# R's sums, T2, T3 and the order of the last quads: who computes them and when

## The chip, the cores and the metric

The kernel runs on one core of a Trainium2 chip. Its engines work side by side and follow each other through semaphores: TensorE (PE; its weight loads are listed apart as PEld) multiplies matrices and writes into PSUM, VectorE (DVE), ScalarE (ACT) and GpSimd (POOL) compute element by element, and SyncE (SP) issues most of the transfers between the main memory and SBUF. Each engine takes its instructions strictly in the order in which the program gives them. The metric is the device time of one execution in microseconds, lower being better. For the kernel before it is 489.55 us, the median of three runs (489.38 to 489.99).

## What is computed

128 samples x of 64 channels and 1024 positions each pass through four layers of a modulated convolution, and the input is added again at the end. Cut to its core the reference is

```python
TYPES = ('same', 'upsample', 'same', 'downsample')
BLUR_K = np.array([1., 3., 3., 1.]); BLUR_K /= BLUR_K.sum()

def _layer(x, style, w, b, mw, mb, typ):
    s = style @ mw.T + mb                                # a scale for each sample and input channel
    weight = SCALE * w * s[:, None, :, None]
    demod = lax.rsqrt(jnp.sum(weight * weight, axis=(2, 3)) + EPS)
    weight = weight * demod[:, :, None, None]            # each sample has weights of its own
    if typ == 'same':
        out = jax.vmap(_conv_same)(x, weight) + b[None, :, None]
    elif typ == 'upsample':                              # transposed, stride 2, then a blur
        out = jax.vmap(_conv_up)(x, weight.transpose(0, 2, 1, 3)) + b[None, :, None]
        out = _blur(out, 2.0 * blur_k, (1, 1))
    elif typ == 'downsample':                            # a blur, then stride 2
        out = jax.vmap(_conv_down)(_blur(x, blur_k, (2, 2)), weight) + b[None, :, None]
    return out

out = x
for i, typ in enumerate(TYPES):
    out = _layer(out, style, weights[i], biases[i], mod_w[i], mod_b[i], typ)
return x + out
```

All arithmetic is float32. There is no nonlinearity between the layers.

## The kernel before, in words

**The mathematics.** As the layers are linear, the kernel multiplies them together into one filter of nine taps of 64x64 for each sample, and applies it once. It does so for a *quad* of four samples at a time; 128 samples make 32 quads (NQ). The 128 partitions hold two samples of 64 channels, and two such pairs lie side by side.

**The chain of the weights.** For each quad, TensorE and ScalarE make the filter in three stages. `stage1` (L408; in the loop `stage1_a` and `stage1_b`, L423 and L435) makes S, `stage2` (L522, with `stage2_rest`, L497) makes R, seven blocks of 64 columns, and `stage3` (L628; in the loop `stage3_b` and `stage3_a`, L593 and L615) makes W, the nine taps. After `stage2`, `r_sums` (L587) adds two pairs of R's blocks into slots 7 and 8 of the R tile; the last group of products of `stage3_b` reads these two slots, the other six groups don't. `combine_a` and `combine_b` (L670, L678) form merged taps H from W by five additions with two SBUF inputs (`sum_of`, all with line L663) and the residual's two (L660).

**The convolution.** The input of a quad comes as three planes X (positions by their remainder by three). From X come the differences G (`in_g01`, `in_g2`, L663), from X directly T3 (`in3`, L712), and from G the operands T1 (`in1`, L727), T2 (`in2`, L732) and the pair T0 and T4, called T04 below (`in04`, L741). Five products of 3 groups each (`conv0` to `conv4`, all L754) turn T and W or H into sums in PSUM: conv3 uses T3, conv1 T1, conv2 T2, conv4 and conv0 T04. conv3, conv1 and conv2 of a quad accumulate in one tile psA, and what is between them is read by the others: `copy_m3` (ScalarE, L793) after conv3, `sum1` (VectorE, L663, y) after conv1, `sum2` (VectorE) after conv2. The first step of `sum2` writes into Y, two instructions of L663, on which conv4 accumulates; its second is y (L813). `output` (L831 on ScalarE, L833 on VectorE) scales and adds the bias, `store` (L836) writes out.

**The buffers.** X has two buffers, used by even and odd quads. G has one. T04, T12 (T1 and T2 in one tile) and T3 have two each, R has two.

**The loop.** Four quads go through `early_turn` (q = 0 to 3), then 25 through `turn_of` (q = 4 to 28), then the last three quads are written out by hand. The order is written out for every engine; nothing is scheduled by a planner. In `turn_of(q)` (L1412) three quads are under way: q is finished, n = q + 1 is begun with conv3 and conv1, and for c = q + 2 the filter and the operands are made. A turn's order is: stage2 of c, conv2 of q, R's sums of c, sum2 of q, T3 of n, stage3_b of c, the first merges of n, conv4 of q, stage3_a, the other merges, conv3 of n, T04 of n, G of c, conv0 of q, conv1 of n, sum1 of n, T1 and T2 of c. The first turn of the loop (q = 4, `entry`) differs: there sum2 and conv4 of q stand ahead of R's sums. Small work for later quads is spread over the turns in tables (`EXTRA`, `TABLES`, `SIDE`, L1250 to L1294), tables of scales on GpSimd among it, and a layered computation of the positions near the two ends of each sample, whose last step is `rest3_bias` (L1106).

**Who does what around the change.** R's sums are on VectorE, T1, T2 and T3 in the loop on GpSimd, T04 and G on VectorE. The loads of X for quad c + 1 are issued by SyncE right behind T3 of n, the last reader of that buffer of X. The two that matter most are

```python
1421            conv2(q)
1422            r_sums(c)
1423            sum2(q)
1424            in3(n, eng=nc_g)
...
1473        sum1(n)
1474        in1(c, nc_g)
1475        in2(c, nc_g)
```

Of the kernel before, what the change touches and what calls it, by code (L numbers as in the profile page):

```python
# [50 lines left out]
ALU = mybir.AluOpType  # L51
# [12 lines left out]
def kernel(  # L64
# [9 lines left out]
    nc = tc.nc  # L74
    NP, P, NXC = x.shape
    B = 2 * NP
    NQ = B // 4
    HB = B // 2
    NT = 9
    T, Bo = slice(0, C), slice(C, P)  # L80
    HALF = (T, Bo)

    nc_v, nc_a, nc_g = nc.vector, nc.scalar, nc.gpsimd
# [35 lines left out]
    bb = par_s[:, NM + N1 + NL : PS]  # L119
# [42 lines left out]
    Xe = const.tile([P, B, 8], F32, name="Xe")  # L162
# [423 lines left out]

    def r_sums(q):  # L587
        t = chain[q]
        nc_v.tensor_add(t[:, :, 7:9], t[:, :, 2:6:3], t[:, :, 3:7:3])  # L589

    shared_w = {}

# [69 lines left out]
    def sum_of(out, x, f, y, op=ALU.add):  # L662
        nc_v.scalar_tensor_tensor(out, x, f, y, op0=ALU.mult, op1=op)  # L663
# [22 lines left out]
    NJ = NB + 2  # L686
# [4 lines left out]
    BOTH_PAIRS = slice(0, 2)  # L691
    PAIR = slice(0, 1), slice(1, 2)

    def plane(buf, i, pairs=BOTH_PAIRS):

        at = PL * (2 - i) if i < 3 else PL * 2 + 1
        return buf[:, pairs, at : at + NJ]

    def t_tile(q, tag):
        if (q, tag) not in Ts:  # L700
            Ts[q, tag] = tpool.tile([P, 2, 1 + (tag != "T3"), PL], F32, tag=tag, name=f"{tag}_{q}")
        return Ts[q, tag]

    def g_tile(q):
        if q not in Gs:
            Gs[q] = gpool.tile([P, 2, 3 * PL], F32, tag="G", name=f"G{q}")
        return Xs[q % NX], Gs[q]

    def in3(q, pairs=BOTH_PAIRS, eng=nc_v):
        if q < NQ:  # L710
            X, t = Xs[q % NX], t_tile(q, "T3")
            eng.tensor_sub(t[:, pairs, 0, :NJ], plane(X, 3, pairs), plane(X, 1, pairs))  # L712

    def in_g01(q, pairs=BOTH_PAIRS):
        if q < NQ:
            X, g = g_tile(q)
            sum_of(g[:, pairs, PL:], X[:, pairs, : 2 * PL], 0.5, X[:, pairs, PL:], ALU.subtract)

    def in_g2(q, pairs=BOTH_PAIRS):
        if q < NQ:  # L720
            X, g = g_tile(q)
            sum_of(plane(g, 2, pairs), plane(X, 3, pairs), 0.5, plane(X, 2, pairs), ALU.subtract)

    def in1(q, eng):
        if q < NQ:
            t, g = t_tile(q, "T12"), Gs[q]
            eng.tensor_add(t[:, :, 0, :NJ], plane(g, 2), plane(g, 1))  # L727

    def in2(q, eng):
        if q < NQ:  # L730
            t, g = t_tile(q, "T12"), Gs[q]
            eng.tensor_sub(t[:, :, 1, :NJ], plane(g, 2), plane(g, 1))  # L732

    def in04(q, pairs=BOTH_PAIRS):
        if q < NQ:
            t, g = t_tile(q, "T04"), Gs[q]
            a, b = g[:, pairs, :NJ], g[:, pairs, 2 * PL : 2 * PL + NJ]
            both = lambda v, step: bass.AP(
                v.tensor, v.offset, [*(list(d) for d in v.ap[:-1]), [step, 2], [1, NJ]]
            )  # L740
            nc_v.tensor_sub(t[:, pairs, :, :NJ], both(a, PL), both(b, 1))  # L741

    def product(q, m, ps, groups=range(K)):

        W, H_ = Wq[q]
        tag, i = SLOT[m]
        for g in groups:
            for s, rows in enumerate(HALF):
                for c, cols in enumerate(HALF):
                    if m in (0, 4):  # L750
                        w = W[rows, tap(m // 2, g), c, :]
                    else:
                        w = H_[rows, m - 1, g, c, :]
                    nc.tensor.matmul(  # L754
                        ps[s][cols, :NB],
                        w,
                        Ts[q, tag][rows, c, i, g : g + NB],
                        start=(g == 0 and m == 3),
                        stop=(g == K - 1),
                        skip_group_check=True,  # L760
                    )

    def m_tile(tag, q, bufs=1):
        return mpool.tile([P, 2, NB], F32, tag=tag, name=f"{tag}_{q}", bufs=bufs)
# [3 lines left out]
    def parts(q):  # L768

        if isinstance(A[q], list):  # L770
            return [(slice(s, s + 1), A[q][s][:, None, :NB]) for s in range(2)]
        return [(slice(0, 2), A[q][:, :, :NB])]

    def banks(q):
        return A[q] if isinstance(A[q], list) else [A[q][:, s] for s in range(2)]
# [22 lines left out]
    def sum1(q):  # L798

        y1w[q] = m_tile("y1", q, 2)  # L800
        for s, a in parts(q):
            sum_of(y1w[q][:, s], a, 2.0, m3c[q][:, s])
# [12 lines left out]
    def conv4(q, *groups):  # L815
        product(q, 4, Y_banks, groups or range(K))

    def conv0(q, *groups):
        product(q, 0, banks(q), groups)
# [15 lines left out]
    def store(q, s, planes=slice(0, K), queue=nc.sync):  # L835
        queue.dma_start(  # L836
            out[q, :, s, planes.start * NB : planes.stop * NB],
            os[q][:, s, planes].rearrange("c i j -> c (i j)"),
        )
# [105 lines left out]
    Oe = const.tile([P, B, 3], F32, name="Oe")  # L945
# [17 lines left out]
    def blurred(g, src, k1, k3, part):  # L963

        for b, f in list(enumerate((k1, k3, k3, k1)))[2 * part : 2 * part + 2]:
            dst = g[:, b : b + K, :]
            nc_v.scalar_tensor_tensor(dst, src, f, dst, op0=ALU.mult, op1=ALU.add)
# [11 lines left out]
    def setup1(part):  # L979
        blurred(g1, woi[1], 0.25, 0.75, part)  # L980
# [34 lines left out]
    def add0(s):  # L1015
        dst = Ye[s][:, :, 1:7]
        nc_v.tensor_tensor(dst, dst, spread(c0, 6), op=ALU.add)
# [85 lines left out]
                op1=ALU.mult,  # L1103
            )

    def rest3_bias():  # L1106

        for rows, xs in ((T, slice(1, 4)), (Bo, slice(4, 7))):
            nc_v.scalar_tensor_tensor(  # L1109
                Oe[rows], Oe[rows], bb[rows, 3:4], Xe[rows, :, xs], op0=ALU.add, op1=ALU.add  # L1110
            )
        nc.sync.dma_start(out_ends, Oe.rearrange("c b j -> c (b j)"))


    PART = slice(0, 16), slice(16, 32), slice(32, B)
# [130 lines left out]
    def layers(i, j):  # L1246
# [31 lines left out]
        10: setup0,  # L1278
        11: lambda: add0(0),
        12: lambda: add0(1),  # L1280
        13: lambda: (setup1(0), setup1(1)),
        15: setup3,
        16: lambda: rest1_bias(0),
        17: lambda: rest1_bias(1),
# [7 lines left out]
        26: lambda: blur_side(0, 2),  # L1292
        27: lambda: blur_side(1, 2),
    }  # L1294

    def extra(*at):
        EXTRA.get(at, lambda: None)()

    def side(work, q):
        work.get(q, lambda: None)()  # L1300
# [111 lines left out]
    def turn_of(q):  # L1412
        n, c, s = q + 1, q + 2, q + 4
        entry = q == FIRST
        stage2(c)
        if entry:
            sum2(q)
            conv4(q)
            r_sums(c)
        else:  # L1420
            conv2(q)
            r_sums(c)
            sum2(q)
            in3(n, eng=nc_g)
        side(TABLES, q)
        for i in range(3):
            load(c + 1, slice(i, i + 1))
        stage3_b(c, open_a(n))
        combine_a(n)
        if entry:  # L1430
            conv0(q, 0, 1)
        else:
            conv4(q)
        stage3_a(c)
        combine_b(n)
        conv3(n)
        if entry:
            copy_m3(n)
        outputs(q, 2)
        if s < NQ:  # L1440
            stage1_a(s)
        if not entry:
            copy_m3(n)
        in04(n)
        if sharing(q):
            share_sums(c + 1)
        in_g2(c)
        side(SIDE, q)
        if q in SMALL:
            l, bs = SMALL[q]  # L1450
            nc_v.memset(high(bs.stop - bs.start), 0.0)
        conv0(q, *((2,) if entry else range(K)))
        if entry:
            conv1(n, 0, 1)
        outputs(q, 1)
        if s < NQ:
            stage1_b(s)
        in_g01(c)
        if sharing(q):
            share(c + 1, banks(q))  # L1460
            share_copy(c + 1)
        outputs(q, 0)
        if q in SLOTS:
            matmuls, width, rest = SLOTS[q]
            slot(matmuls, width, Y_banks)
            rest()
        if s == NQ:
            slot(ends3, 3, unit(ps_w, "psE"), 3)
            rest3()
        if q in SMALL:  # L1470
            small(q)
        conv1(n, *((2,) if entry else range(K)))
        sum1(n)
        in1(c, nc_g)
        in2(c, nc_g)
        if s + 1 < NQ:
            scale3(s + 1)

# [5 lines left out]
    q, n, c = NQ - 3, NQ - 2, NQ - 1  # L1484
    stage2(c)
    conv2(q)
    in3(n, eng=nc_g)
    stage3(c, 0)
    sum2(q, (0,))
    combine_a(n)  # L1490
# [3 lines left out]
    conv3(n)  # L1494
    outputs(q, 2)
    copy_m3(n)
    rest3_bias()
    in04(n)
    in3(c)
    in_g01(c)  # L1500
    stage3(c, 1)
    conv0(q, 0)
    conv1(n)
    outputs(q, 1)
    in_g2(c)
    sum1(n)
    combine_a(c)
    combine_b(c, (0,))
# [10 lines left out]
    q, n = NQ - 2, NQ - 1  # L1519
# [10 lines left out]
        store(q, i, slice(1, K))  # L1530
    in04(n, PAIR[0])
    in04(n, PAIR[1])
    conv0(q, 0)
    conv2(n)
    conv0(q, 1, 2)
# [5 lines left out]
    q = NQ - 1  # L1541
    for i, queue in enumerate((nc.sync, nc_a)):
        output(q, 1, i, nc_v)
        store(q, i, slice(1, 2), queue)
    conv4(q)
    for i, (eng, queue) in enumerate(zip(BOTH, (nc.sync, nc_a))):
        output(q, 2, i, eng)
# [83 lines left out]
```

## Time and profile before

| | us |
|---|---|
| median of three runs | 489.55 (489.38 to 489.99) |
| the profiled execution's own time | 488.37 |
| its span in the trace | 486.6 |
| TensorE busy | 472.5 |
| VectorE busy | 396.2 |
| ScalarE busy | 310.7 |
| GpSimd busy | 186.6 |
| granted TensorE clock, share of full | 0.999 |

Rows of the profile read as follows. In the order of time: start and duration in us, engine, line, operation, the names of what is written and read (buffer numbers left out, so that W, H and T of different quads have one name), shape, count, and in brackets how long the engine stood idle before it and who released it. In the list of waits: who waited for whom, total us, number of times, the longest. A row for one line: shortest, median and longest duration in ns, the first and last start in us, the shape. "POOL" is GpSimd, "DVE" VectorE. A row can merge several instructions of one kind ("x24"), and its duration is then that of the group. Small bits of matrix work are pipelined, so the ends of products are modelled, while the weight loads (PEld) show when TensorE really went on.

### The profile page before, as it was taken

The page shows a single profiled execution, that of the slowest core. Times are in us where ns is not written, and L with a number is a line of the kernel's source. Part 1 is how long each engine was busy: PE and PEld are TensorE (multiplying, and loading weights), DVE is VectorE, ACT ScalarE, POOL GpSimd, SP SyncE. Part 2 cuts the span into 40 slices and gives each one's busy share as a digit, 9 for nine tenths or more (in the row PEclk, how much of TensorE's full clock was granted, in tenths as well). Part 3 has the DMA queues.
Part 4 walks back from the last instruction along what each step waited for, and adds up shares of the span by engine and source line. Part 5 has one row for each costly group of instructions (what it writes and reads, how often), then busy time and mean ns, then how long its engine had stood idle before and what let it go on. Part 6 is the DMA issues. An engine that isn't in the chain of part 4 may idle for free. (4 is left out here: it accounts for less than half of the span.)

```text
span 486.6 us, 26761 instructions
## 1 busy us (share of the span) xinstructions
PE 472.5 (97%) x11928; PEld 343.2 (71%) x11928; DVE 396.2 (81%) x688; ACT 310.7 (64%) x708; POOL 186.6 (38%) x198
## 2 busy tenths in 40 slices
PE   8999999999999999999999999999999999999975
PEld 7877788767677766977776666767676667666742
DVE  4789998687978887988868988869888888898694
ACT  5465666667666676766666766667766677766432
POOL 3434132754345444134443144441344443333300
PEclk9999999999999999999999999999999999999999
DMA  7216364445355445455544355444555445545224
GB/s 246 60 47 205 110 209 165 148 119 175 120 148 166 133 154 167 134 153 155 144 152 147 107 164 162 132 149 145 148 149 152 131 161 175 154 148 155 75 76 172
DMA packets 50498, 70.70 MB, mean 145 GB/s; under 512 B 5648, under 2 KB 47312, under 8 KB 50384
## 3 DMA queue, kind: packets, MB, share of 16 engines
q1 hardware_dynamic: 49792, 68.32, 45.2%
q8 instruction: 93, 1.52, 1.4%
q10 hardware_dynamic: 592, 0.69, 0.5%
q14 instruction: 21, 0.17, 0.1%
HBM read 35.36 MB, written 33.62 MB: 142 GB/s over the span
## 5 line engine op out<-in xcount | busy, mean ns | idle before, releaser
L754 PE MATMUL psA<-T,H 64*64 64x340 f32 x2304 | 185.9, 447 | 2.9 <-DVE y L663 2.7
L754 PEld LDWEIGHTS psA<-T,H 64*64 64x64 f32 x2304 | 88.4, 133 | 52.4 <-DVE y L663 4.7
L446 POOL TENSOR_TENSOR S<-S 128x128 f32<-128x128 f32 x28 | 20.6, 735 | 162.4 <-ACT S L361 162.3
L663 DVE SCALAR_TENSOR_TENSOR G<-X 128x1376 f32<-128x1376 f32 (+2 forms) x65 | 78.0, 1205 | 0.2
L727 POOL TENSOR_TENSOR T<-G 128x684 f32<-128x684 f32 x28 | 46.5, 1659 | 74.4 <-DVE G L663 71.8
L754 PE MATMUL Y<-T,Wf 64*64 64x340 f32 x768 | 62.5, 452 | 3.0 <-DVE Y L663 2.1
L361 ACT ACTIVATE R<-psR,tC 128x448 f32<-128x448 f32 x63 | 36.6, 631 | 44.0 <-PE psR L468 26.4
L754 PE MATMUL psA<-T,Wf 64*64 64x340 f32 x768 | 63.5, 446 | 0.0
L589 DVE TENSOR_TENSOR R<-R 128x256 f32<-128x256 f32 x25 | 21.0, 839 | 51.9 <-ACT R L361 51.9
L361 ACT ACTIVATE Wf<-psW,t 128x256 f32<-128x256 f32 (+2 forms) x76 | 32.7, 480 | 32.6 <-PE psW L572 32.3
L361 ACT ACTIVATE psW<-psA 128x128 f32<-128x128 f32 x100 | 19.4, 268 | 49.6 <-PE psA L572 45.4
L741 DVE TENSOR_TENSOR T<-G 128x1368 f32<-128x1368 f32 (+1 forms) x33 | 50.8, 1543 | 0.0
L468 PE MATMUL psR<-S,E 64*64 64x64 f32 (+1 forms) x1472 | 46.6, 238 | 0.0
L732 POOL TENSOR_TENSOR T<-G 128x684 f32<-128x684 f32 x28 | 46.3, 1655 | 0.0
L754 PEld LDWEIGHTS Y<-T,Wf 64*64 64x64 f32 x768 | 28.7, 132 | 24.4 <-DVE Y L663 7.9
L712 POOL TENSOR_TENSOR T<-X 128x684 f32<-128x684 f32 x25 | 44.7, 1788 | 0.0
L390 PEld LDWEIGHTS psS<-wd,w2n 64*64 64x64 f32 x1120 | 34.1, 133 | 14.5 <-ACT S L361 0.8
L468 PEld LDWEIGHTS psR<-S,E 64*64 64x64 f32 x1472 | 39.6, 134 | 5.6 <-ACT psR L491 0.7
L831 ACT ACTIVATE o<-psA,tb,td 128x340 f32<-128x340 f32 x63 | 37.1, 648 | 6.3 <-PE psA L754 6.3
L831 ACT ACTIVATE o<-Y,tb,td 128x340 f32<-128x340 f32 x63 | 36.7, 638 | 4.6 <-PE Y L754 2.7
L754 PEld LDWEIGHTS psA<-T,Wf 64*64 64x64 f32 x768 | 28.3, 133 | 15.6
L663 DVE SCALAR_TENSOR_TENSOR Y<-m,psA 128x340 f32<-128x340 f32 x64 | 32.8, 512 | 7.7 <-PE psA L754 6.4
(164 smaller groups left out, 853.0 us busy)
## 6 DMA issues: line engine op xcount, KB each, us to landing
out<-o SPq DMA_DIRECT2D x167, 170.0 KB, 2.6
X<-in_x SPq DMA_DIRECT2D x150, 172.0 KB, 3.2
X<-in_x SPq DMA_DIRECT2D x14, 516.0 KB, 5.2
out<-o SPq DMA_DIRECT2D x6, 510.0 KB, 5.8
out<-o SPq DMA_DIRECT2D x2, 340.0 KB, 2.7
Xe<-in_x_ends SPq DMA_DIRECT2D x1, 512.0 KB, 6.7
out<-o ACTq DMA_DIRECT2D x3, 170.0 KB, 2.6
par<-in_params SPq DMA_DIRECT2D x2, 192.0 KB, 4.2
```

The costliest lines, as they stand in the source:

```text
L361: nc_a.activation(dst, src, AF.Copy, scale=f)
L390: nc.tensor.matmul(ps[r][cols, at * C : (at + n) * C], weight[rows], wd[c if r == 0 else 1 - c][rows, taps], start=first, stop=last, skip_ ...
L446: nc_g.tensor_add(t[:, :, 2], t[:, :, 2], t[:, :, 0])
L468: nc.tensor.matmul(dst[r][cols], weight[rows], st[c if r == 0 else 1 - c][rows, slots, :], start=False, stop=last, skip_group_check=True,)
L589: nc_v.tensor_add(t[:, :, 7:9], t[:, :, 2:6:3], t[:, :, 3:7:3])
L663: nc_v.scalar_tensor_tensor(out, x, f, y, op0=ALU.mult, op1=op)
L712: eng.tensor_sub(t[:, pairs, 0, :NJ], plane(X, 3, pairs), plane(X, 1, pairs))
L727: eng.tensor_add(t[:, :, 0, :NJ], plane(g, 2), plane(g, 1))
L732: eng.tensor_sub(t[:, :, 1, :NJ], plane(g, 2), plane(g, 1))
L741: nc_v.tensor_sub(t[:, pairs, :, :NJ], both(a, PL), both(b, 1))
L754: nc.tensor.matmul(ps[s][cols, :NB], w, Ts[q, tag][rows, c, i, g : g + NB], start=(g == 0 and m == 3), stop=(g == K - 1), skip_group_check ...
L831: nc_a.activation(dst, src, AF.Identity, bias=add, scale=d3)
```

## The change

R's sums go from VectorE to GpSimd. T2, which GpSimd computed last in a turn, is computed by GpSimd behind R's sums in the next turn. T3, which GpSimd computed there, is computed by VectorE behind sum1 at the end of the turn before. In turn 13 one of the two halves of `setup1` (two additions each) moves behind T3. T04 of the last quad but one is computed at the end of the last turn of the loop instead of in the part written by hand. There VectorE's order becomes G, then T3, then sum1, and the bias of the ends, `rest3_bias`, with its store is cut in two halves that are placed later.

```diff
     def r_sums(q):
         t = chain[q]
-        nc_v.tensor_add(t[:, :, 7:9], t[:, :, 2:6:3], t[:, :, 3:7:3])
+        nc_g.tensor_add(t[:, :, 7:9], t[:, :, 2:6:3], t[:, :, 3:7:3])
...
-    def in3(q, pairs=BOTH_PAIRS, eng=nc_v):
+    def in3(q, pairs=BOTH_PAIRS):
         if q < NQ:
             X, t = Xs[q % NX], t_tile(q, "T3")
-            eng.tensor_sub(t[:, pairs, 0, :NJ], plane(X, 3, pairs), plane(X, 1, pairs))
+            nc_v.tensor_sub(t[:, pairs, 0, :NJ], plane(X, 3, pairs), plane(X, 1, pairs))
...
-    def rest3_bias():
-
-        for rows, xs in ((T, slice(1, 4)), (Bo, slice(4, 7))):
-            nc_v.scalar_tensor_tensor(
-                Oe[rows], Oe[rows], bb[rows, 3:4], Xe[rows, :, xs], op0=ALU.add, op1=ALU.add
-            )
-        nc.sync.dma_start(out_ends, Oe.rearrange("c b j -> c (b j)"))
+    def rest3_bias(half):
+
+        rows, xs = ((T, slice(1, 4)), (Bo, slice(4, 7)))[half]
+        nc_v.scalar_tensor_tensor(
+            Oe[rows], Oe[rows], bb[rows, 3:4], Xe[rows, :, xs], op0=ALU.add, op1=ALU.add
+        )
+        nc.sync.dma_start(out_ends[rows], Oe[rows].rearrange("c b j -> c (b j)"))
...
-        13: lambda: (setup1(0), setup1(1)),
+        13: lambda: setup1(0),
...
+    LATE = {13: lambda: setup1(1)}
...
             conv2(q)
             r_sums(c)
             sum2(q)
-            in3(n, eng=nc_g)
+            in2(n, nc_g)
         side(TABLES, q)
...
         sum1(n)
+        in3(c)
+        side(LATE, q)
+        if s == NQ:
+            in04(c)
         in1(c, nc_g)
-        in2(c, nc_g)
         if s + 1 < NQ:
             scale3(s + 1)
...
     q, n, c = NQ - 3, NQ - 2, NQ - 1
     stage2(c)
     conv2(q)
-    in3(n, eng=nc_g)
+    in2(n, nc_g)
     stage3(c, 0)
...
     copy_m3(n)
-    rest3_bias()
-    in04(n)
+    in_g01(c)
+    in_g2(c)
     in3(c)
-    in_g01(c)
     stage3(c, 1)
     conv0(q, 0)
     conv1(n)
     outputs(q, 1)
-    in_g2(c)
     sum1(n)
...
     in04(n, PAIR[0])
     in04(n, PAIR[1])
+    rest3_bias(0)
     conv0(q, 0)
...
         output(q, 1, i, nc_v)
         store(q, i, slice(1, 2), queue)
+    rest3_bias(1)
     conv4(q)
```

## The prediction

> **What bounds the kernel now.** I began with the page's first part and went from there to the waits of the weight loads, which show TensorE's stops most sharply.
>
> ```profile
> PE 472.5 (97%) x11928; PEld 343.2 (71%) x11928; DVE 396.2 (81%) x688; ACT 310.7 (64%) x708; POOL 186.6 (38%) x198
> ```
> ```profile
> PEld Y L754 <- DVE Y L663: 7.9, 19, 0.8
> PEld psA L754 <- DVE y L663: 4.7, 5, 3.1
> ...
> PEld psR L468 <- ACT psR L491: 0.7, 2, 0.5
> PEld psA L572 <- DVE R L589: 0.6, 1, 0.6
> ```
>
> TensorE sets the pace. VectorE, though 81% busy, matters only where TensorE stops for it, and the stops named are few: conv4 waits 19 times for Y, the result of the first half of sum2; conv2 waits once for 3.1 us for y, the result of sum1; the last products of stage3_b wait once for R's sums. The change touches all three. What holds Y up shows in the order of time within one turn:
>
> ```profile
> 425.13 1.63 POOL L732 TENSOR_TENSOR T<-G 128x684 f32<-128x684 f32 x1
> 426.27 0.98 PEld L572 LDWEIGHTS psA<-R,w0s 64*64 64x64 f32 x24
> 426.30 0.75 DVE L589 TENSOR_TENSOR R<-R 128x256 f32<-128x256 f32 x1 [2.20 <-ACT R L361]
> ...
> 426.97 1.05 DVE L663 SCALAR_TENSOR_TENSOR Y<-m,psA 128x340 f32<-128x340 f32 x2
> ...
> 427.60 0.21 PEld L572 LDWEIGHTS psA<-R,par 64*64 64x64 f32 x8
> ...
> 428.08 1.35 PEld L754 LDWEIGHTS Y<-T,Wf 64*64 64x64 f32 x24 [0.26 <-DVE Y L663]
> ...
> 428.71 0.55 DVE L663 SCALAR_TENSOR_TENSOR H<-Wf 128x384 f32<-128x384 f32 x1
> ...
> 437.24 0.85 DVE L663 SCALAR_TENSOR_TENSOR y<-psA,m 128x680 f32<-128x680 f32 x1
> ...
> 437.49 1.65 POOL L727 TENSOR_TENSOR T<-G 128x684 f32<-128x684 f32 x1 [2.67 <-DVE G L663]
> ```
> ```profile
> 252.99 0.54 DVE L589 TENSOR_TENSOR R<-R 128x256 f32<-128x256 f32 x1 [2.21 <-ACT R L361]
> 253.49 1.07 DVE L663 SCALAR_TENSOR_TENSOR Y<-m,psA 128x340 f32<-128x340 f32 x2
> ```
> ```profile
> L589 DVE TENSOR_TENSOR R<-R x25: 426/792/1906, 93.3 to 440.3; 128x256 f32<-128x256 f32 x25
> ```
>
> The same sum of R takes from 0.43 to 1.91 us. In the turn shown GpSimd's T2 runs until 425.13 + 1.63 = 426.76, and R's sum ends at 427.05, 0.29 us after it: VectorE adding two SBUF operands stands still while GpSimd works, and of the 0.43 us that it takes alone 0.29 are left once GpSimd is done, so 0.14 is start-up. Y is queued behind it, starts 0.67 us after R's sum did, and conv4 starts 1.11 us after Y. In the turn at 252.99, where R's sum is short, Y starts 0.50 us after it; that is as early as Y can be, because then it waits for conv2 itself.
>
> **The change part by part.**
>
> *R's sums to GpSimd.* Y then starts when conv2 ends, at 0.50 instead of 0.67 in the turn shown: 0.17 us saved of a wait of 0.26, so 0.09 us of each listed wait stays. The 19 waits hold one from the tail (0.71 us, shown below); 18 with 7.2 us are left. With the 0.6 us for R this is 7.8, and less 18 times 0.09 it is **6.2 us**. All 7.8 would be the upper end. The sum itself must be ready for the last product group, loaded at 427.60, 1.30 us after R is there. GpSimd has not run this shape. Its 128 elements take 0.46 us (95.05 below), its 684 take 1.65 (437.49), so 256 are about 0.73 by the line through both; the bounds are 0.46 and 1.65. I take 0.73: ready at 0.8, half a microsecond early. GpSimd's T1 in front of it ends at 437.49 + 1.65 = 439.14; R comes after VectorE's 2.20 us of idle time behind sum1, at about 440.3, so the queue is free.
>
> *T3 to VectorE behind sum1, T2 into the next turn.* T3 costs 0.86 us on VectorE (463.22 below). It lies in the 2.20 us of idle time behind sum1, and even if it stands behind GpSimd's T1 until 439.14 it ends near 439.9, with sum2 due at 440.8. Without that cover it would cost its 0.86 us a turn. T2 has a whole turn before conv2 reads it. It now follows R's sum, so it runs until some 2.5 us after R and can hold up VectorE's first merge (428.71, at 2.24 in the new order) by 0.2 us; conv3 sits behind conv4 and stage3_a, so I count nothing and leave 2 us over all turns to the range. The loads of X are released earlier, since T3 was the last reader of the old X. GpSimd's queue holds no DMAs. On GpSimd T2 and, in two turns, tables now queue behind R's sum, whose wait is for ScalarE's R; VectorE waits for T2 before it overwrites G, but only after six merges (0.55 each) and T04.
>
> *The first turn of the loop.* Here GpSimd isn't free. Its backlog of small table work stands ahead of R's sum:
>
> ```profile
> 93.32 0.63 POOL L885 TENSOR_TENSOR c0f<-dm,par_s 128x96 f32<-128x96 f32 x1
> 93.91 1.19 POOL L458 TENSOR_TENSOR wsq<-E 128x128 f32<-128x128 f32 x2
> 95.05 0.46 POOL L459 TENSOR_TENSOR wsq<-E 128x128 f32<-128x128 f32 x1
> ```
> ```profile
> 90.64 0.85 DVE L813 TENSOR_TENSOR y<-y,psA 128x680 f32<-128x680 f32 x1
> 93.32 0.43 DVE L589 TENSOR_TENSOR R<-R 128x256 f32<-128x256 f32 x1 [1.82 <-ACT R L361]
> 93.66 0.70 DVE L663 SCALAR_TENSOR_TENSOR H<-Wf 128x384 f32<-128x384 f32 x1
> ...
> 97.64 1.77 DVE L741 TENSOR_TENSOR T<-G 128x1368 f32<-128x1368 f32 x1
> 99.50 0.87 DVE L663 SCALAR_TENSOR_TENSOR G<-X 128x684 f32<-128x684 f32 x1
> ```
> ```profile
> 94.66 0.24 PEld L572 LDWEIGHTS psA<-R,par 64*64 64x64 f32 x8
> ```
>
> TensorE needs the sum at 94.66. If GpSimd keeps its pace, the backlog ends at 95.51, the sum at 96.2, and TensorE stops for **1.6 us**. But VectorE, which waited 1.82 us for R, no longer waits: its merges start at 91.5, and it runs ahead into T04 (1.58 us unhindered, 461.72 below) and G (0.87), all with two SBUF operands. The rows show that the exclusion works both ways and in turn: c0f took 0.63 us beside R's sum, and the two of L458 took 1.19 where two at 0.46 make 0.92. So each GpSimd operation may stand behind one of VectorE's. Taking away the 0.6 us of such waits that the old order had, GpSimd with the sum would end at 95.6. Against that stand five merges at 0.42 (2.1), T04 at 1.44, G at 0.72 (each less 0.14 us of start-up), 4.3 us in all; about eight starts of GpSimd's own, taken as 0.14 each too, overlap them, which leaves 3.2. The sum is then ready at 98.8: **4.1 us** lost. The bounds are 1.6 and 5.2 (nothing overlaps). I take 4.1, because VectorE has nothing else to wait for. Everything behind it is relative to TensorE and shifts with it.
>
> *The weight sums of turn 13, split over two places.*
>
> ```profile
> L967 DVE SCALAR_TENSOR_TENSOR g<-par,g x4: 358/359/611, 230.5 to 231.9; 128x192 f32<-128x192 f32 x4
> ```
> ```profile
> 233.06 0.41 PEld L468 LDWEIGHTS psR<-S,E 64*64 64x64 f32 x6 [0.49 <-ACT psR L491]
> ```
>
> Four of them delay the chain that this load waits for; two, about 0.9 us, go behind T3 into idle time. The wait of 0.49 goes: **0.5 us**, at least 0.
>
> *The last quads.*
>
> ```profile
> 455.60 1.07 DVE L663 SCALAR_TENSOR_TENSOR Y<-m,psA 128x340 f32<-128x340 f32 x2 [3.28 <-PE psA L754]
> ...
> 460.45 1.24 DVE L1109 SCALAR_TENSOR_TENSOR Oe<-Oe,par_s,Xe 64x384 f32<-64x384 f32 x2
> 461.72 1.58 DVE L741 TENSOR_TENSOR T<-G 128x1368 f32<-128x1368 f32 x1
> 463.22 0.86 DVE L712 TENSOR_TENSOR T<-X 128x684 f32<-128x684 f32 x1
> 464.00 2.37 DVE L663 SCALAR_TENSOR_TENSOR G<-X 128x1376 f32<-128x1376 f32 x2
> 466.29 0.86 DVE L663 SCALAR_TENSOR_TENSOR y<-psA,m 128x680 f32<-128x680 f32 x1
> ```
> ```profile
> 461.64 1.90 PE L754 MATMUL psA<-T,H 64*64 64x340 f32 x24
> ```
> ```profile
> 467.20 1.35 PEld L754 LDWEIGHTS psA<-T,H 64*64 64x64 f32 x24 [3.11 <-DVE y L663]
> ...
> 477.98 1.35 PEld L754 LDWEIGHTS Y<-T,Wf 64*64 64x64 f32 x24 [0.71 <-DVE Y L663]
> ```
>
> Ahead of sum1 (466.29) VectorE now has the ends' bias (1.24) and T04 (1.58); both leave, 2.8 us. conv1 ends at 461.64 + 1.90 = 463.5, so sum1 can move to 463.6 and conv2 from 467.20 to 464.5: **2.7 us**. T04 goes into the 3.28 us before 455.60: T3 0.86 and T04 1.58 make 2.4 and fit, unless both stand behind GpSimd's T2, so at least 2.1 us stay. The bias halves (0.62 each) and the two stores on SyncE's queue that replace one go into gaps nearer the end; the first just fits ahead of the last sum2, 0.1 us at most.
>
> **Sum:** 6.2 + 0.5 + 2.7 - 4.1 = 5.3 us. The profiled execution of 488.37 us becomes 483.1; the median of the runs, 489.55, lies 1.2 above it and becomes **484.3**.
>
> **The rivals.** *A, the first turn is milder:* GpSimd keeps its pace, 1.6 lost instead of 4.1: 481.8. For it speaks that VectorE's merges are short; against it that T04 and G come in one piece.
>
> *B, the clock:* a stop of 4 us is longer than any that this trace has in the loop; the longest, 3.11 at 467.20, is followed by products at the usual 1.35 us a group. If the clock fell to half for two groups it would cost 2 times 1.35: 487.0. The Trainium skill, TensorE: Matmul & The Clock Gate, section on why this matters for your kernels, advises against gaps of more than about 3 us in TensorE, after which the clock halves; no run here shows it.
>
> *C, the loop's gain is eaten:* T3 behind GpSimd's T1 on VectorE runs past conv2's end, or the later T2 holds the merges up until conv3 waits. At 0.25 us a turn nothing is left of the 6.2, and the sum is 0.5 + 2.7 - 4.1, a time of 490.5, slower. It begins when T3 ends 0.9 us later than worked out and decides at 1.2; for it speaks that R's sum was held by up to 1.5 us by GpSimd, against it the idle 2.20 us.
>
> *D, GpSimd is too slow for R's sum:* conv4 is late once the sum passes 1.2 us; from 1.45 us, 23 turns at 0.23 us take all of the 5.3, and at 1.65, the duration of 684 elements, it would be about 494. The Trainium skill, GPSIMD Engine Reference, section Performance versus the Vector engine, has GpSimd about twice as slow in such additions and says to keep them on VectorE; twice 0.43 is 0.86, which by itself would still be hidden.
>
> **How the numbers follow.** Chances: the forecast 0.56, A 0.23, B 0.07, C 0.09, D 0.05. The forecast's own range goes from 482.7 (all 7.8 in the loop) to 487.0 (5.2 in the first turn, 2.1 in the tail, half of the merges' 2). A is at 481.8, or 480.2 with all 7.8; I start between them at 481.0. B is at the upper end. So 481.0 to 487.0 leaves out C, D and the extremes. About 0.2%, 1 us, can be told from no change: faster 0.86 (forecast, A, B), within 0.04 (half of C), slower 0.10.
>
> **What would show it.** In the changed kernel's profile the waits of weight loads for Y should shrink to below 2 us in the loop and R's sums should never be named outside the first turn; there, near 94.7, one wait for R's sums of about 4 us should stand, its GpSimd row starting near 98. T3's rows on VectorE should lie ahead of each Y with idle time behind them. The 3.11 us before conv2 in the tail should be about 0.4. I am wrong if R's sums take over 1.2 us on GpSimd, if conv3 waits for merges, or if the first turn's wait is absent.

## The result, and the profile after

| | before | after |
|---|---|---|
| median of the runs compared, us | 489.15 (15 runs, 487.87 to 490.71) | 485.56 (15 runs, 484.52 to 488.10) |
| ratio after/before, 95% interval | | 0.9939 [0.9922, 0.9956] |
| the profiled execution's own time, us | 488.37 | 485.29 |
| its span, us | 486.6 | 483.5 |
| VectorE busy, us | 396.2 | 417.6 |
| GpSimd busy, us | 186.6 | 163.9 |
| granted TensorE clock | 0.999 | 0.994 |

The change makes the kernel faster, by 0.4 to 0.8%. The first part of the changed kernel's page and its waits of the weight loads (who waited for whom, total us, times, longest):

```profile
PE 472.4 (98%) x11928; PEld 350.3 (72%) x11928; DVE 417.6 (86%) x688; ACT 310.1 (64%) x708; POOL 163.9 (34%) x198
```
```profile
PEld psA L572 <- POOL R L589: 4.1, 1, 4.1
...
PEld psA L754 <- DVE y L663: 1.6, 4, 0.5
...
PEld Y L754 <- DVE Y L663: 0.7, 1, 0.7
```

The 19 waits for Y are one, in the tail; the 3.1 us before conv2 are gone (the longest for y is 0.5). In their place stands one new wait, 4.1 us for R's sums, in the first turn of the loop. VectorE is busy 21 us more, and in the turn below the added time lies where it was idle.

One turn in the order of time, the same as in the prediction:

```profile
423.23 1.67 POOL L727 TENSOR_TENSOR T<-G 128x684 f32<-128x684 f32 x1 [2.67 <-DVE G L663]
...
423.75 1.87 DVE L712 TENSOR_TENSOR T<-X 128x684 f32<-128x684 f32 x1
...
426.10 0.73 POOL L589 TENSOR_TENSOR R<-R 128x256 f32<-128x256 f32 x1 [1.20 <-ACT R L361]
...
426.53 1.07 DVE L663 SCALAR_TENSOR_TENSOR Y<-m,psA 128x340 f32<-128x340 f32 x2 [0.91 <-PE psA L754]
426.79 1.66 POOL L732 TENSOR_TENSOR T<-G 128x684 f32<-128x684 f32 x1
...
427.34 0.21 PEld L572 LDWEIGHTS psA<-R,par 64*64 64x64 f32 x8
...
427.65 1.35 PEld L754 LDWEIGHTS Y<-T,Wf 64*64 64x64 f32 x24
...
428.28 0.58 DVE L663 SCALAR_TENSOR_TENSOR H<-Wf 128x384 f32<-128x384 f32 x1
...
430.14 0.78 PEld L754 LDWEIGHTS psA<-T,H 64*64 64x64 f32 x16
```

T3 takes 1.87 us instead of its own 0.86, because it stands behind GpSimd's T1: T1 ends at 424.90, T3 0.72 us later, at 425.62. VectorE still waits 0.91 us before Y, so T3 is hidden. R's sum ends at 426.83, half a microsecond before the load at 427.34 that needs it. Y no longer waits for it, and conv4 at 427.65 has no wait in front.

The first turn. Here are its weight loads, the granted clock by stretches (start and end, length, the busy times and counts of PE, PEld, DVE, ACT and POOL, then the clock), GpSimd and VectorE:

```profile
94.25 0.36 PEld L572 LDWEIGHTS psA<-R,w0s 64*64 64x64 f32 x16
98.74 0.21 PEld L572 LDWEIGHTS psA<-R,par 64*64 64x64 f32 x8 [4.13 <-POOL R L589]
...
99.66 0.27 PEld L754 LDWEIGHTS psA<-T,Wf 64*64 64x64 f32 x4 [0.30 <-issue]
```
```profile
92.00:98.70 6.70, 2.75 (x72) 2.09 (x64) 6.44 (x11) 1.11 (x2) 6.44 (x10) 1.00 0.42 128
98.70:102.60 3.90, 3.86 (x56) 2.67 (x60) 0.10 (x1) 1.61 (x6) 1.26 (x4) 0.56 0.00 0
```
```profile
94.73 2.83 POOL L458 TENSOR_TENSOR wsq<-E 128x128 f32<-128x128 f32 x2
97.52 0.47 POOL L459 TENSOR_TENSOR wsq<-E 128x128 f32<-128x128 f32 x1
97.95 0.73 POOL L589 TENSOR_TENSOR R<-R 128x256 f32<-128x256 f32 x1
```
```profile
94.48 1.72 DVE L741 TENSOR_TENSOR T<-G 128x1368 f32<-128x1368 f32 x1
96.30 0.95 DVE L663 SCALAR_TENSOR_TENSOR G<-X 128x684 f32<-128x684 f32 x1
```

GpSimd's backlog is stretched as worked out: two products of L458 take 2.83 us beside T04 and G. But the wait is not all. In the 3.9 us behind it the granted clock is 0.56; the loads come four at a time with 0.30 us of "issue" between, and nothing is late that the profile could name. Read in steps of half a microsecond, the clock is 1.00 through the wait, falls to 0.50 at about 98.9, and is back at 1.00 at about 102.3: one stretch of 3.4 us at half.

To share the time out, these are the starts of conv4's first load in us, by quad, in four traces (the last two are experiments below). Quads 4 and 5 enclose the first turn's loss, 13 and 14 the turn with the weight sums, and 29 and 30 the tail:

| conv4 of quad | before | after | e1_entry_v | e4_loop_only |
|---|---|---|---|---|
| 4 | 91.73 | 91.56 | 93.40 | 92.90 |
| 5 | 108.83 | 113.89 | 109.92 | 109.43 |
| 13 | 224.16 | 227.30 | 223.31 | 223.13 |
| 14 | 239.04 | 241.14 | 237.15 | 237.37 |
| 29 | 456.77 | 456.22 | 452.29 | 452.00 |
| 30 | 470.40 | 467.31 | 463.43 | 465.70 |

After minus before goes from -0.17 (quad 4) to 5.06 (5), falls to -0.55 (29) and steps to -3.09 (30). So the first turn costs over 5 us, the loop pays them back slowly, and the tail is the net gain. Steps alone are compared, since these four traces differ by up to 1.8 us at quad 4.

### The profile page after: what moved, and what is told of

Its sections match the earlier page's. It is cut to its first block, busy times and chain, and to the rows that moved or that the text cites. A ratio compares the mean times of both kernels' runs of the same rounds, so it can differ in the third digit from the quotient of the medians.

```text
span 483.5 us, 26719 instructions
## 1 busy us (share of the span) xinstructions
PE 472.4 (98%) x11928; PEld 350.3 (72%) x11928; DVE 417.6 (86%) x688; ACT 310.1 (64%) x708; POOL 163.9 (34%) x198
## 4 chain that ended last, share of the span: by engine, by line
PE 86%; issue 5%; POOL 4%; DVE 4%; ACT 0%; ACTq 0%; DVEq 0%; POOLq 0%
PE psA L754 41%; PE Y L754 10%; PE psR L468 9%; PE psA L572 7%; PE psW L572 6%; PE psS L390 5%; PE psR L534 3%; PE psA L468 2%; PE Y L995 2%; POOL T L732 1%; POOL T L727 1%; DVE G L663 1%; POOL wsq L458 1%; DVE H L663 1%; PE Y L337 1%
## 5 line engine op out<-in xcount | busy, mean ns | idle before, releaser
L754 PEld LDWEIGHTS psA<-T,H 64*64 64x64 f32 x2304 | 90.8, 133 | 48.0 <-issue 2.2
L446 POOL TENSOR_TENSOR S<-S 128x128 f32<-128x128 f32 x28 | 22.1, 788 | 148.8 <-ACT S L361 148.7
L754 PE MATMUL psA<-T,Wf 64*64 64x340 f32 x768 | 65.0, 453 | 0.0
L712 DVE TENSOR_TENSOR T<-X 128x684 f32<-128x684 f32 x32 | 47.4, 1481 | 0.0
L754 PEld LDWEIGHTS Y<-T,Wf 64*64 64x64 f32 x768 | 29.7, 132 | 17.7 <-DVE Y L663 0.7
L754 PEld LDWEIGHTS psA<-T,Wf 64*64 64x64 f32 x768 | 29.6, 135 | 15.4 <-issue 0.6
L831 ACT ACTIVATE o<-y,tb,td 128x340 f32<-128x340 f32 x62 | 38.5, 678 | 0.6 <-DVE y L813 0.6
```

The source lines that it names most:

```text
L446: nc_g.tensor_add(t[:, :, 2], t[:, :, 2], t[:, :, 0])
L712: nc_v.tensor_sub(t[:, pairs, 0, :NJ], plane(X, 3, pairs), plane(X, 1, pairs))
L754: nc.tensor.matmul(ps[s][cols, :NB], w, Ts[q, tag][rows, c, i, g : g + NB], start=(g == 0 and m == 3), stop=(g == K - 1), skip_group_check ...
L831: nc_a.activation(dst, src, AF.Identity, bias=add, scale=d3)
```

## The experiments

In the theory, GpSimd in the first turn costs a wait of about 4 us and then some 1.5 us of slower clock; the loop gains because nothing of GpSimd's runs when R comes; the tail gains by VectorE's order. The rivals put the loop's gain on VectorE being relieved of R's sums, or the 4 us on GpSimd's backlog alone.

**e1_entry_v: R's sums on VectorE in the first turn only.**

```diff
-    def r_sums(q):
+    def r_sums(q, eng=nc_g):
...
             conv4(q)
-            r_sums(c)
+            r_sums(c, nc_v)
```

> The changed kernel, with R's sums back on VectorE in the first turn of the loop alone. Theory: that turn's 4.13 us wait for R's sums and the half clock behind it (the loads to conv3 took 3.8 us after the wait against 2.3 before) are a pure loss of about 5.6 us; without them the time is 485.56 - 5.6 = 480.0, the granted clock is back at 0.999, and conv4 of turn 5 comes no later than in the kernel before. Rival: VectorE's head start in that turn is worth something, or the loss is partly made up later; then it gains under 3 us (over 482.5).

479.69 us (479.47 to 482.50, 6 runs) against 488.46, ratio 0.9819 [0.9788, 0.9851]. The new wait is gone from its list. This one line gives back 5.9 us of the medians, and the version beats both kernels. By the table, from quad 4 to 5 it steps by -0.58 where the changed kernel steps by +5.23: the first turn's price is 5.81 us, more than the wait.

**e2_hold_v: VectorE waits for R again, GpSimd still makes the sum.** To the changed kernel, behind R's sums of the first turn, VectorE's own addition of R's blocks into a scratch tile is added.

```diff
             r_sums(c)
+            hold = const.tile([P, 2, 2, C], F32, name="hold")
+            nc_v.tensor_add(hold, chain[c][:, :, 2:6:3], chain[c][:, :, 3:7:3])
```

> The changed kernel, but in the first turn of the loop VectorE also adds the same blocks of R into a scratch tile, so that it waits for ScalarE's R there as it did before; the sum that is used stays on GpSimd. Theory: 2.5 of the 4.1 us are GpSimd standing behind VectorE's merges, T04 and G. With VectorE held back GpSimd is done at about 96.2, TensorE waits 1.6 us, and the clock stays full: 485.56 - 2.5 - 1.5 = 481.5. Rival: the wait is GpSimd's own backlog and stays near 4 us, with the half clock: 485.5.

481.79 us, 0.9854 [0.9824, 0.9884]. Its weight loads, GpSimd and the window behind the wait:

```profile
97.06 0.21 PEld L572 LDWEIGHTS psA<-R,par 64*64 64x64 f32 x8 [1.35 <-POOL R L589]
```
```profile
94.55 1.37 POOL L458 TENSOR_TENSOR wsq<-E 128x128 f32<-128x128 f32 x2
...
96.29 0.73 POOL L589 TENSOR_TENSOR R<-R 128x256 f32<-128x256 f32 x1
```
```profile
98.00:102.00 4.00, 4.00 (x100) 2.71 (x92) 3.84 (x6) 2.77 (x9) 1.39 (x3) 1.00 0.01 4
```

An instruction that only makes VectorE wait for R cuts TensorE's stop from 4.13 to 1.35 us. So of the 4.13 us, 2.78 are VectorE running ahead, and 1.35 are the backlog. L458 takes 1.37 us instead of 2.83, which is 1.46 of the 2.78; the rest lies in the small rows ahead of it, which stood beside VectorE's merges in the changed kernel (its two tables of L285 take 0.53 and 0.74 us here, 0.94 and 1.12 there). The clock stays at 1.00 after the short stop.

**e10_busy: TensorE kept at work through the wait.** To the changed kernel 28 products with a zero weight are added, ahead of the group that needs R's sums, in the first turn.

```diff
+            if i == len(plan) - 1:
+                zeros_to_y(fill, NB, False)
...
-        stage3_b(c, open_a(n))
+        stage3_b(c, open_a(n), 14 if entry else 0)
```

> The changed kernel with 28 products of zeros (added to Y, about 3.5 us of TensorE's time) ahead of the last group of stage3_b in the first turn of the loop, where TensorE would wait for R's sums. Theory: the half clock behind that wait comes from TensorE standing still for 4 us; kept busy, TensorE goes on at full clock, and 1.5 us come back although more work is done: 485.56 - 1.5 = 484.1, granted clock 1.00 behind the wait. Rival: the clock falls for another reason (the burst after the wait), or the slow products are not the clock's: 485.5, or later if the zeros delay the last group.

484.10 us (483.78 to 484.50), 0.9877 [0.9845, 0.9909]: 1.46 below the changed kernel's median.

```profile
95.34 3.67 PEld L181 LDWEIGHTS Y<-Z 64*64 64x64 f32 x56
99.61 0.21 PEld L572 LDWEIGHTS psA<-R,par 64*64 64x64 f32 x8 [0.59 <-POOL R L589]
```
```profile
98.70:102.60 3.90, 3.90 (x84) 2.42 (x79) 0.94 (x2) 2.15 (x8) 2.13 (x6) 1.00 0.00 0
```

The sum is as late as in the changed kernel, yet the clock stays at 1.00 and the stretch behind it runs at its usual pace. Beside the kernel before, conv4 steps by 3.66 us from quad 4 to 5 (92.42 to 113.18) where the changed kernel steps by 5.23, so the trace has 1.57 us back. Work that computes nothing makes the kernel faster, and what differs behind the wait is the clock.

**e3_only_entry: to the kernel before, the first turn's part alone.** R's sums by GpSimd in that turn, all else as before.

```diff
             conv4(q)
-            r_sums(c)
+            r_sums(c, nc_g)
```

> The kernel before, with R's sums on GpSimd in the first turn of the loop alone. Theory: the whole loss of 5.6 us and nothing else: 489.15 + 5.6 = 494.8, a wait of about 4.1 us and a granted clock near 0.55 for about 3.5 us behind it. Rival: the loss is made up later in a kernel that has slack in its other waits: under 492.

494.82 us (493.77 to 496.38), 1.0121 [1.0087, 1.0155]. Its list and, from the tail, the loads of conv2 and the window there:

```profile
PEld psA L572 <- POOL R L589: 4.1, 1, 4.1
```
```profile
473.33 0.21 PEld L754 LDWEIGHTS psA<-T,H 64*64 64x64 f32 x8 [3.13 <-DVE y L663]
473.76 0.26 PEld L754 LDWEIGHTS psA<-T,H 64*64 64x64 f32 x4 [0.23 <-issue]
474.33 0.26 PEld L754 LDWEIGHTS psA<-T,H 64*64 64x64 f32 x4 [0.30 <-issue]
```
```profile
475.00:478.50 3.50, 3.50 (x40) 1.71 (x36) 1.77 (x5) 0.00 (x0) 0.00 (x0) 0.72 0.00 0
```

The 4.1 us wait stands without the rest of the change, and from quad 4 to 5 conv4 steps by 5.60 us (91.28 to 113.98). And the trace shows what the profile of before did not: there the old wait of 3.11 us was followed by loads at the usual pace, here 3.13 us are followed by loads in fours and a clock of 0.72. The window behind the wait in the kernel before:

```profile
467.20:470.00 2.80, 2.80 (x40) 1.61 (x44) 2.58 (x7) 0.00 (x0) 0.00 (x0) 1.00 0.03 8
```

A wait of that length costs clock in one trace and not in another. In steps of half a microsecond, the tail of e3 has the clock at 0.50 from about 473.6 to 477.0, and its first turn from about 98.1 to 101.5: 3.4 us each time, as in the changed kernel.

**e4_loop_only: to the kernel before, the loop's part alone.** VectorE keeps the sums in the first turn; the weight sums and the tail stay, but for T2 of the last turn, which follows there.

```diff
             conv2(q)
-            r_sums(c)
+            r_sums(c, nc_g)
             sum2(q)
-            in3(n, eng=nc_g)
+            in2(n, nc_g)
...
         sum1(n)
+        in3(c)
         in1(c, nc_g)
-        in2(c, nc_g)
```

> The kernel before with the loop's part alone: from the second turn on R's sums on GpSimd, T2 behind them, T3 on VectorE behind sum1; the first turn, the weight sums of turn 13, and the last quads stay. Theory: the waits of conv4 for Y in the loop go, 5.1 to 6.2 us: 489.15 - 5.6 = 483.5. Rival: part of the 5.6 us that the changed kernel gained over its loop is the recovery of what the first turn lost; then it gains under 4 us (over 485).

483.81 us, 0.9894 [0.9864, 0.9924]. By the table it goes from +1.17 at quad 4 to -4.77 at quad 29: 5.94 us gained. Of the waits for Y only the tail's is left in its list, "0.7, 1", as in the changed kernel. The tail's wait for sum1 is still there, listed under "issue", with 3.19 us before conv2 and a clock of 1.00 behind it:

```profile
PEld psA L754 <- issue: 5.1, 8, 3.2
```

From quad 13 to 14 it gains 0.64, the changed kernel 1.04; the 0.40 between them are the split of the weight sums.

**e5_tail_only: to the kernel before, the last quads' part alone.** The edit is that of the change for the tail (T04 of the last quad but one in the last turn, G and T3 ahead of sum1, `rest3_bias` in halves).

```diff
+        if s == NQ:
+            in04(c)
...
-    rest3_bias()
-    in04(n)
-    in3(c)
     in_g01(c)
+    in_g2(c)
+    in3(c)
```

> The kernel before with the last quads' part alone: T04 of the last quad but one at the end of the loop, G and T3 straight ahead of sum1, the bias of the ends in two later halves. Theory: conv2's 3.11 us wait for sum1 shrinks to about 0.4, 2.5 to 2.7 us: 489.15 - 2.6 = 486.5. Rival: T04 at the end of the loop, behind T1, T2 and T3 on GpSimd, which all stand in this kernel, delays sum2 and gives half of it back: over 487.5.

485.20 us, 0.9900 [0.9868, 0.9933], against 489.85 for the kernel before on that chip. In the trace conv4 of quad 30 steps by -2.61 us, as in the changed kernel (-2.54). The rest of the 4.65 is not in this trace. Of those 13 runs of the kernel before, 10 had a mean clock of 0.994 to 0.996 and a median of 489.95; the three at 0.999 or 1.000 had 487.92, 488.46 and 489.01. All four runs of this kernel had 0.998 or more, with a median 3.3 us below that 488.46; what makes the 0.7 us between 3.3 and 2.6 is open.

**e11_tail_busy: is it the tail's clock that spreads the runs of before?** To the kernel before, 22 zero products ahead of conv2 in the tail.

```diff
+    zeros_to_y(11, NB, False)
     conv2(n)
```

> The kernel before with 22 products of zeros (added to Y, about 2.9 us of TensorE's time) ahead of conv2 of the last quad but one, where TensorE waits 3.11 us for sum1. Theory: that wait lies at the edge of what lets the clock fall; in some runs of the kernel before it falls there and costs 1.7 us, which is why its runs lie at 487.9 to 488.4 or at 489.1 and more. With TensorE kept busy the runs keep to the lower group: median 488.2 or lower, beside 489.15. Rival: the two groups have another cause, and the median stays at 489 or rises.

488.54 us (488.18 to 489.37, 12 runs) against 489.36 (487.39 to 491.16, 17 runs), 0.9990 [0.9975, 1.0005]: no difference shown.

```profile
464.53 3.28 PEld L181 LDWEIGHTS Y<-Z 64*64 64x64 f32 x44
467.68 3.56 PEld L754 LDWEIGHTS psA<-T,H 64*64 64x64 f32 x48
```

Conv2 starts 0.48 us later than before (467.20), so the filler has a price. What did change is the clock: 0.997 or more in all 12 runs, where 11 of the 17 of before had 0.997 or less. The runs of before sort by it: the six with 0.999 or more have a median of 488.05, the eleven others 489.67. The version with the filler lies 0.49 above the six, which is the filler's price. That fits a clock lost behind the tail's wait in most runs of before; where those runs lost it was not traced, and a gain in time is not shown.

**e6_t2_stays: the version of e1 with T2 in its old place,** at the end of the turn before, so R's sums follow it on GpSimd.

```diff
             sum2(q)
-            in2(n, nc_g)
...
         in1(c, nc_g)
+        in2(c, nc_g)
```

> The changed kernel with the first turn's R's sums on VectorE (479.7), but T2 stays on GpSimd behind T1 at the end of a turn. Theory: T2's move is what makes R's sums early enough. T1, T3 on VectorE and T2 follow each other because of the shared access, T2 ends about 3.9 us after T1's start, R's sums about 4.65, that is 1.85 us after R is there instead of 0.8, past the 1.30 where the products want them; conv4 about 0.5 us late in each of 23 turns: 490, with R's sums on GpSimd named among TensorE's waits. Rival: the queue has room, and T2's place doesn't matter: 479.7 to 481.

487.34 us, 0.9950 [0.9934, 0.9967]: 7.7 us above e1, where some 10 were expected. Its waits, and GpSimd in one turn:

```profile
PEld psA L572 <- POOL R L589: 7.6, 20, 0.8
```
```profile
427.45 2.28 POOL L732 TENSOR_TENSOR T<-G 128x684 f32<-128x684 f32 x1
429.69 0.72 POOL L589 TENSOR_TENSOR R<-R 128x256 f32<-128x256 f32 x1
```

Now TensorE waits for R's sums in 20 turns. T2 is held by VectorE's T3 and takes 2.28 us, and the sum queues behind it. Without T2's move, the sums on GpSimd return more than the loop gains.

**e7_gate: who must add?** The version of e1, but VectorE makes R's sums in every turn, and GpSimd, ahead of T2, only adds one column of each of R's blocks into a scratch tile, which makes it wait for R.

```diff
-            r_sums(c)
+            r_sums(c, nc_v)
+            t = chain[c]
+            nc_g.tensor_add(hold[:, :, :, :1], t[:, :, 2:6:3, :1], t[:, :, 3:7:3, :1])
             sum2(q)
             in2(n, nc_g)
```

> The changed kernel with R's sums on VectorE in all turns, while GpSimd only adds 4 columns of R into a scratch tile before T2, so that it still starts T2 no sooner than R is there. Theory: what held Y up was GpSimd at work beside VectorE's sum, not the 0.43 us of the sum; with GpSimd held back VectorE has the sum done before conv2 ends, and the time is that of the version with only the first turn mended, 479.7 to 481. Rival: VectorE had to be rid of the sum; then Y comes 0.2 us later in each turn: over 484.

480.14 us (479.70 to 481.44), 0.9805 [0.9765, 0.9845]; e1 has 0.9819 [0.9788, 0.9851]. It makes no difference that can be told which engine adds. VectorE's sum now takes 0.41 to 0.43 us in all 25 turns, where in the kernel before it took up to 1.91. What gains is that T2 does not run when R comes.

**e8_twice: R's sums cost twice as much on GpSimd.** The version of e1, with the same addition made first into a scratch tile in each turn.

```diff
+            t = chain[c]
+            nc_g.tensor_add(hold, t[:, :, 2:6:3], t[:, :, 3:7:3])
             r_sums(c)
```

> The changed kernel with the first turn's R's sums on VectorE (479.7), but in all later turns GpSimd adds R's blocks twice, first into a scratch tile, so that the sums are ready about 1.5 us after R instead of 0.8. Theory: the products want them at 1.30, so conv4 comes 0.2 to 0.3 us later in each of 24 turns, 5 to 7 us in all: 485.5, with R's sums named among TensorE's waits in most turns. Rival: there is more room than 0.5 us, and 0.73 us more of GpSimd costs nothing: under 481.

492.69 us, 1.0076 [1.0056, 1.0097]: a miss. It is 13.0 us above e1, 0.54 us in each of 24 turns. One turn, on GpSimd, VectorE and TensorE's loads (lines are shifted by 2: L734 is T2, L756 the convolution):

```profile
432.77 0.73 POOL L589 TENSOR_TENSOR R<-R 128x256 f32<-128x256 f32 x1
433.46 1.64 POOL L734 TENSOR_TENSOR T<-G 128x684 f32<-128x684 f32 x1
```
```profile
434.21 1.31 DVE L665 SCALAR_TENSOR_TENSOR H<-Wf 128x384 f32<-128x384 f32 x1
```
```profile
433.55 0.21 PEld L572 LDWEIGHTS psA<-R,par 64*64 64x64 f32 x8 [0.18 <-POOL R L589]
...
436.62 1.38 PEld L756 LDWEIGHTS psA<-T,H 64*64 64x64 f32 x24 [0.27 <-issue]
```

The sum is 0.18 us late, as expected. Not foreseen was T2 behind it: it runs until 435.10 and holds VectorE's first merge for 1.31 us (0.58 in the changed kernel), and conv3 then waits as well: 0.27 us, listed under "issue", until just behind the merge that it reads, which ends at 436.50.

**e9_t3_gps: the version of e1 with T3 still on GpSimd,** between R's sums and T2.

```diff
-            nc_v.tensor_sub(t[:, pairs, 0, :NJ], plane(X, 3, pairs), plane(X, 1, pairs))
+            eng.tensor_sub(t[:, pairs, 0, :NJ], plane(X, 3, pairs), plane(X, 1, pairs))
...
             sum2(q)
+            in3(n, eng=nc_g)
             in2(n, nc_g)
...
         sum1(n)
-        in3(c)
```

> The changed kernel with the first turn's R's sums on VectorE (479.7), but T3 stays on GpSimd, between R's sums and T2. Theory: GpSimd has the time for it; what it costs is only that T3 and T2 together stand in the way of VectorE's merges until 4.1 us after R instead of 2.5. The three merges ahead of conv3 are each held back once, 0.3 us or more beyond their slack: 479.7 + 24 times 0.2 = 484, with conv3 waiting for H. Rival: the merges have the slack, and T3's move to VectorE is worth nothing: under 480.5.

508.36 us, 1.0399 [1.0380, 1.0418]: a large miss. The waits, GpSimd, VectorE and TensorE's loads in one turn:

```profile
PEld psA L754 <- POOL T L732: 24.3, 22, 1.1
```
```profile
446.98 1.66 POOL L712 TENSOR_TENSOR T<-X 128x684 f32<-128x684 f32 x1
448.58 1.97 POOL L732 TENSOR_TENSOR T<-G 128x684 f32<-128x684 f32 x1
```
```profile
448.97 1.85 DVE L660 SCALAR_TENSOR_TENSOR Wf<-idn,t,Wf 128x64 f32<-128x64 f32 x2
450.86 0.56 DVE L663 SCALAR_TENSOR_TENSOR H<-H,Wf 128x384 f32<-128x384 f32 x1
```
```profile
451.54 1.38 PEld L754 LDWEIGHTS psA<-T,H 64*64 64x64 f32 x24 [1.11 <-POOL T L732]
```

The list names T2, but conv3 does not read T2, and T2 ends at 450.55, a microsecond before the load. What conv3 reads is the merge that ends at 451.42, and that stood behind the residual of L660, held for 1.85 us by GpSimd. So where T3 runs makes 28.7 us between these two versions (508.36 less 479.69).

## Why the prediction was right, and where it was off

The forecast was 484.3, the measured median 485.56: inside the range, on the right side, 1.3 us above. The profiled execution fell by 3.1 us (488.37 to 485.29) where the sum said 5.3, so in the trace the forecast was 2.2 us too good. That the median lies closer is luck: 1.2 us were added from the profiled execution to the median, and in the changed kernel that step is 0.27. Term by term:

| term (us gained) | forecast | measured |
|---|---|---|
| loop | 6.2 | 5.75 to 5.94 (e1 from quad 4 to 29, 1.67 to -4.48, less the 0.40 below; e4) |
| weight sums of turn 13 | 0.5 | 0.40 |
| tail | 2.7 | 2.54 |
| first turn | -4.1 | -5.81 (5.23 + 0.58) |

With 5.75 in the loop the measured terms make 2.9; the other 0.2 of the 3.1 is the start (-0.17 at quad 4).

**The first turn is the step that was off, in its size.** Its wait was forecast at 4.1 us and is 4.13; its place and the start of the sum near 98 are right too, and e2 confirms the working: 1.35 us for the backlog alone (1.6 forecast) and the rest from VectorE's run ahead. But the term stopped at the wait. The prediction had the clock as rival B, with a chance of 0.07 and 2.7 us, and left it out of the sum. It was granted at 0.56 for 3.9 us. From the load that had waited to that of conv3 it is 3.81 us here (98.74 to 102.55) and 2.26 before (94.66 to 96.92), 1.55 us more. e10 takes the clock's part away and leaves the sum as late, and is 1.46 us faster by the medians and 1.57 by the traces. So the wait of the forecast and the mechanism of B both came, the latter at about half its price. The changed kernel's other runs may pay more: the nine with a mean clock of 0.994 to 0.996 took 484.52 to 485.67 us, the six with 0.990 to 0.992 took 486.15 to 488.10. One of the nine was profiled, so where the six lose their clock stays open; e10, without the stop, had 0.997 or more and 483.78 to 484.50 in all four runs. What spoke against B was the wait of 3.11 us in the tail (which the prediction counts to the loop), and it left the clock alone in that one trace; e3 shows that such a wait can also cost it.

The Trainium skill, TensorE: Matmul & The Clock Gate, Part 1, has the clock at half after at least one idle window of about 3.4 us, and has that window free-running. The rows agree in part: 4.1 us cost the clock in two traces (0.56, and 0.57 in e3), and 1.35 us did not. But 3.13 us, shorter than that window, cost it in e3, while 3.11 us (before) and 3.19 us (e4) did not; here the measurement decides.

**The loop** gained 0.3 to 0.5 us less than forecast. In the turn worked out in the prediction the step is 0.16 us (428.08 to 427.65, after 414.08 to 413.81 a turn earlier), with 0.17 forecast. Where the small rest lies was not traced turn by turn. The duration of 256 elements on GpSimd, 0.73 by the line through two other sizes, is 0.726 in the middle of 25:

```profile
L589 POOL TENSOR_TENSOR R<-R x25: 723/726/898, 97.9 to 439.9; 128x256 f32<-128x256 f32 x25
```

T3 is hidden, and T3 behind T1 ended where it should: 0.72 us behind T1's end, which is 0.86 less the 0.14 of start-up. The Trainium skill, SBUF — State Buffer, section Who interferes with whom, says that a VectorE instruction with two SBUF inputs contends with a GpSimd instruction that reads SBUF, over a shared port pair that is an exclusive lock; T3's 1.87 us here and L458's 2.83 in the first turn agree with it.

But one reading in the loop was incomplete. The prediction had the gain come from R's sums leaving VectorE. e7 shows that it comes with VectorE still making them, so long as T2 waits for R, and e6 that it goes when T2 stays. The gain belongs to T2's new place, with T3 out of GpSimd's way; which engine adds matters little. How much T3's move would give alone, with R's sums on VectorE and T2 in its old place, was not run.

**The counted-nothing step, T2 against the merges,** held by a narrow margin: 0.58 us instead of 0.55 for the first merge, and conv3 without a wait. Rival C, the merges held until conv3 waits, did not come true, but e8 and e9 show how near it was. With T2 0.7 us later (e8) a turn cost 0.54 us more, which leaves a slack of about 0.2 (in the turn shown of the changed kernel, the merge that conv3 reads ends at 429.85 and its load starts at 430.14; in e8 and e9 the load follows the merge by 0.12); with T3's 1.66 us in front of T2 (e9) it cost 1.2 (28.7 over 24 turns). Rival D's price (0.23 us a turn for a sum that takes 1.45) was too low for the same reason: it looked at the sum alone, and not at what is queued behind it on GpSimd.

**The tail** is as forecast. VectorE's T04 is where it was put, and sum1 starts when conv1 ends:

```profile
453.37 1.57 DVE L741 TENSOR_TENSOR T<-G 128x1368 f32<-128x1368 f32 x1
...
462.20 0.87 DVE L712 TENSOR_TENSOR T<-X 128x684 f32<-128x684 f32 x1
463.12 0.87 DVE L663 SCALAR_TENSOR_TENSOR y<-psA,m 128x680 f32<-128x680 f32 x1
```
```profile
464.11 3.10 PEld L754 LDWEIGHTS psA<-T,H 64*64 64x64 f32 x48 [0.57 <-issue]
```

Conv2's wait fell from 3.11 to 0.57 us. That this also takes a cause of clock loss out of the runs is likely by e3, e5 and e11, but a time for it is not shown.

## What to carry to other kernels

When two engines hold each other up, as VectorE and GpSimd do here, ask which operation is running at the moment when the critical one becomes ready: holding the uncritical one back until then can be worth as much as moving the critical one elsewhere. A steady-state move should be costed again for the first turn, where queues are not empty and where an engine that lost its wait runs ahead into the other's way. And a stop of TensorE of 3 us or more can have two prices, the wait and the slower clock behind it; look at the granted clock behind such a stop in more than one execution before putting it at nothing.

## What the runs showed of the hardware

- A stop of 4.13 us brought a granted clock of 0.56 over the next 3.9 us and cost about 1.5 us; one of 1.35 us cost none; stops of 3.11 and 3.19 us were followed by 1.00 and one of 3.13 by 0.72. In all three places where the clock fell, it stood at 0.50 for 3.4 us.
- Keeping TensorE at work on products of zeros through such a stop kept the clock at 1.00 and made the kernel 1.46 us faster.
- A wait that does no work, put on VectorE, took 2.78 us off the stop. GpSimd's rows ahead of the sum were shorter beside the waiting VectorE: 1.37 us instead of 2.83 for the same two products of L458, and 0.53 instead of 0.94 for the first of the two tables.
- VectorE's residual of 64 elements a row, two instructions that take 0.47 us unhindered, took 1.85 us behind GpSimd's T2 of 1.97: they were held for three times their own time.
